# Layer 1 of two attention layers: where the maxima are turned, and how the last two chunks are summed

## The chip, the cores and the metric

One core of one Trainium2 chip runs the whole kernel. The metric is the device time of one execution in microseconds; the figure to compare is the median of several executions. In every profile PE is the matrix engine (PEld its weight loads), DVE the vector engine, ACT the scalar engine, POOL the GpSimd engine, and SP the engine that issues most DMAs. L905 means line 905 of the kernel before.

## What is computed

The input is x of shape (2, 256, 64, 64), in float32. Two attention layers follow each other. Layer 0 normalises, attends with 4 heads of 16, scales and passes through a sigmoid; the change does not touch it. Layer 1 is:

```python
def _L1_conv_ref(x, w_qkv, b_qkv, w_out, b_out):
    b, c, h, w = x.shape
    head_dim = c // HEADS                     # 4 heads of 64
    qkv = jnp.einsum('oc,bchw->bohw', w_qkv, x) + b_qkv[None, :, None, None]
    qkv = qkv.reshape(b, HEADS, 3 * head_dim, h * w)
    q, k, v = jnp.split(qkv, 3, axis=2)
    attn = jax.nn.softmax(jnp.einsum('bhdn,bhdm->bhnm', q, k) * scale, axis=-1)
    out = jnp.einsum('bhnm,bhdm->bhnd', attn, v).reshape(b, c, h, w)
    return jnp.einsum('oc,bchw->bohw', w_out, out) + b_out[None, :, None, None] + x
```

There are 4096 positions for each of 2 images, so each head has a score matrix of 4096 by 4096.

## The kernel before

**Units, steps, chunks.** Layer 1 is cut into 32 units. A unit is one image, one pair of heads and one block of 512 queries. It goes over all 4096 keys in 32 chunks of 128 keys, two chunks a step, so a unit has 16 steps, numbered 0 to 15 here, and layer 1 has 512 steps. One tile of a chunk is 128 keys by 1024: 512 queries for each of the two heads.

**The life of a chunk.** `score` multiplies keys by queries into a pair of PSUM banks (L888; two such pairs). `keep` takes the running maximum over chunks on DVE (`rmax`, L905) and copies the scores to an SBUF tile `raw` on ACT (L906). The tiles `raw` are a ring of 26 buffers. Eleven steps later (`LAG`) `shift` subtracts the queries' maxima on DVE (L977), `weigh` takes the exponential on ACT (L989) and adds the weights into a running total on POOL (L1001; L999 for the first two chunks of a half). A step after that `gather` multiplies the weights by the values on PE (L1030). A buffer of the ring is free for chunk t+26 once POOL's addition and PE's weighing of chunk t are over.

**Halves and maxima.** The 32 chunks are two halves of 16, and each half has a maximum of its own. When a half is complete (step 8 for the first, step 0 of the next unit for the second) `turn_max` transposes `rmax` on PE, one head at a time, into the single spare bank `misc` (L918), and `fold` reduces it on DVE (L935), sends it to DRAM and reads it back, spread over all partitions, as a row. `place_shift` copies the row into PSUM on ACT (L959) two steps later. One chunk of each half is shifted by POOL instead of DVE (L966).

**Sums.** POOL adds 30 of the 32 chunks of a unit. The last two are summed by PE: `gather` of the last chunk multiplies both by ones (L1043), in step 11 of the next unit, into two column groups of the spare bank. `total` in step 12 adds POOL's two totals to the same bank (L1060): the first half into column groups at 0 and 32, the second half onto the last chunks at 64 and 96. `keep_total` copies the bank out in step 13 (L1068) and sends it through DRAM with five DMAs, so that it comes back with queries on partitions. `add_sums` on POOL multiplies the first half by the ratio of the two maxima's exponentials (L1151) and adds the second (L1152). `factors` and `rows` turn the sums into factors and apply them in steps 0 and 1 of the unit after.

**Projections beside it.** The first 24 units also project keys and values that a later pair of heads needs, a quarter at a time: keys in steps 2 to 5, values in steps 6, 7, 9 and 10 (`next_values`, L835), kept by `store_values` on ACT (L844) in steps 8 and 11. The last eight units do the output projection in the same places (`project_out`, `output`, L812, L1200), with two additions on POOL (L1206). Queries of the next unit are projected in steps 13 and 14. All of these, the turned maxima and the sums share the one spare bank.

**What sets the order.** The order is written by hand. A table maps a step and a place to calls (`at`, run by `hung`), and the main loop runs the places of a step in this order: scores of both chunks, exponential left from the step before, `start`, `early`, keep of the first chunk, shift and exponential of an older chunk, `early end`, keep of the second chunk, weighing of two chunks, `late`, `late end`, shift of the second older chunk, `end`. Every engine works through its own instructions in that order. The main loop before:

```python
            scores = [score(c) for c in pair] if inside else []
            if 0 <= t - LAG - 1 < END:
                weigh(pair[1] - 2 * LAG - 2)
            hung(t, "start")
            hung(t, "early")
            if inside:
                keep(pair[0], scores[0])
```

Of the kernel before, what the change touches and what calls it, by code (L numbers as in the profile page):

```python
# [8 lines left out]
F32 = mybir.dt.float32  # L9
AF = mybir.ActivationFunctionType  # L10
ALU = mybir.AluOpType
# [3 lines left out]
P = 128  # L15
# [11 lines left out]
def conv_attention_kernel(  # L27
# [205 lines left out]
    with own0:  # L233
# [417 lines left out]
        def misc(name):  # L651
            return small_bank[0](name)
# [118 lines left out]
    with (  # L771
# [26 lines left out]
        sum1 = {  # L798
            u: dram.tile([NG * 2, NB], F32, tag="sum_{}_{}_{}".format(*u), name=f"sum_{u}")
            for u in units  # L800
        }
        first, begun, late = {}, set(), {}


# [217 lines left out]
        def gather(t):  # L1022
            u = b, g, j = units[t // NM]
            m = t % NM
            n = m // GS
            if m % GS == 0:
                avs1[u, n] = psv.tile([P, NB], F32, tag="av", name=f"av1_{b}_{g}_{j}_{n}")
            v = vs[b, g, m // PB]
            for k in range(2):
                seq(nc.tensor.matmul(  # L1030
                    avs1[u, n][k * D1 : (k + 1) * D1, :], v[:, m % PB, k, :], raws[t][:, k, :],
                    start=(m % GS == 0), stop=(m % GS == GS - 1),
                ))
            if on_tensor(t) and t % 2 == 1 and t != 2 * END - 1:
                late_sums((t - 1, t) if on_tensor(t - 1) else (None, t))
            elif t == 2 * END - 2:
                late_sums((t, t + 1))
            if m == NM - 1 and u != units[-1]:
                srows[u] = misc(f"sum1_{b}_{g}_{j}")
                for i in (t - 1, t):  # L1040
                    for k in range(2):
                        r = D1 * (NG - 1) + 32 * k
                        seq(nc.tensor.matmul(  # L1043
                            srows[u][r : r + 32, :], ones[:, :32], raws[i][:, k, :],
                            start=(i < t), stop=False, skip_group_check=True,
                        ))
            raws.pop(t - 2, None)
            if m % GS == GS - 1:
                a = l1.tile([P, NB], F32, tag="avs", name=f"avs1_{b}_{g}_{j}_{n}")
                seq(nc.scalar.copy(a, avs1.pop((u, n))))  # L1050
                avs1[u, n] = a

        def total(u):


            b, g, j = u
            for n in range(NG):
                for k in range(2):
                    r = D1 * n + 32 * k
                    seq(nc.tensor.matmul(  # L1060
                        srows[u][r : r + 32, :], ones[:, :32], accs[u, n][:, k, :],
                        start=(n < NG - 1), stop=True, skip_group_check=True,
                    ))

        def keep_total(u):
            b, g, j = u
            row = l1.tile([P, NB], F32, tag="kv", name=f"srow_{b}_{g}_{j}")
            seq(nc.scalar.copy(  # L1068
                row.rearrange("p (a m i) -> p a i m", m=P, i=2),
                srows[u].rearrange("p (a i m) -> p a i m", m=P, i=2),  # L1070
            ))
            for m in range(2 * NG):
                nc.sync.dma_start(out=sum1[u][m : m + 1, :], in_=row[32 * m : 32 * m + 1, :])
            s = small.tile([P, NG, 2, PB], F32, tag="sums1", name=f"sums1_{b}_{g}_{j}")
            nc.sync.dma_start(
                out=s.rearrange("p n k (a i) -> p (n k a) i", i=2),
                in_=sum1[u].rearrange("m (a p i) -> p (m a) i", p=P, i=2),
            )
            srows[u] = s
# [141 lines left out]

        for n, u in enumerate(units):
            b, g, j = u
            t0 = n * US
# [6 lines left out]
            if n < len(units) - NJ:  # L1233
                to = (*units[n + NJ][:2], j)
                at(max(t0 - 1, 0), "start", lambda to=to: fetch(("kv", *to), x1[to[0]][to[2]]))
                for q in range(4):
                    at(t0 + 2 + q, "late", lambda to=to, q=q: next_keys(*to, q))
                    at(t0 + (6, 7, 9, 10)[q], "late", lambda to=to, q=q: next_values(*to, q))
                at(t0 + 6, "start", lambda to=to: store_keys(*to))
                for i, step in enumerate((t0 + 8, t0 + 11)):  # L1240
                    at(step, "start", lambda to=to, i=i: store_values(*to, i))

                t1 = (n // NJ * NJ + NJ - 1) * US
                at(t1 + 2 * j + 2, "start", lambda to=to: load_keys(*to))
                at(t1 + 2 * j + 3 + LAG, "start", lambda to=to: load_values(*to))
            for k in range(NG):
                t1 = t0 + (k + 1) * GS // 2
                places = ("early", "early" if (u, k) == (units[-1], NG - 1) else "late")
                for i, place in enumerate(places):
                    at(t1, place, lambda u=u, k=k, i=i: turn_max(u, k, i))  # L1250
                    at(t1, f"{place} end", lambda u=u, k=k, i=i: fold(u, k, i))
                at(t1 + 2, "end", lambda u=u, k=k: place_shift(u, k))
            t1 = t0 + US + GS // 2
            if u != units[-1]:
                at(t1 + 4, "late", lambda u=u: total(u))
                at(t1 + 5, "start", lambda u=u: keep_total(u))
                at(t1 + 1, "late", lambda u=u: lose(u))
                at(t1 + 7, "late end", lambda u=u: add_sums(u))
                at(t1 + 8, "end", lambda u=u: factors(u))
                for place, k in (("early", 1), ("late", 0)):  # L1260
                    at(t1 + 9, place, lambda u=u, k=k: turn_sums(u, k))
                    at(t1 + 9, f"{place} end", lambda u=u, k=k: rows(u, k))
            else:
                at(END + 1, "late", lambda u=u: last_lost(u))
                at(END + 4, "early", lambda u=u: late_sums((None, None)))
                at(END + 4, "early end", lambda u=u: keep_late(0))
                at(END + 5, "early", lambda u=u: turn_late(0))
                at(END + 5, "early end", lambda u=u: add_late(u, 0))
                at(END + 6, "early", lambda u=u: turn_sums(u, 0))
                at(END + 6, "early end", lambda u=u: first_rows(u))  # L1270
                at(END + LAG, "late", lambda u=u: turn_late(1))
                at(END + LAG, "late", lambda u=u: add_late(u, 1))
                at(END + LAG, "late", lambda u=u: turn_sums(u, 1))
                at(END + LAG, "late", lambda u=u: last_rows(u))
            if n >= len(units) - NJ:
                b0 = B - 2
                at(t0 - 1, "start", lambda b0=b0, j=j: fetch_output(b0, j))
                for o in range(CC):
                    for q in range(4):
                        step = t0 + ((2, 3, 4, 5), (6, 7, 9, 10))[o][q]  # L1280
                        at(step, "late", lambda b0=b0, j=j, o=o, q=q: project_out(b0, j, o, q))
                at(t0 + 6, "start", lambda b0=b0, j=j: output(b0, j, 0, 2))
                for part, step in enumerate((t0 + 8, t0 + 11)):
                    at(step, "start", lambda b0=b0, j=j, part=part: output(b0, j, 1, part))


# [77 lines left out]
        for t in range(max(t for t, _ in extras) + 1):  # L1364
            inside, behind = 0 <= t < END, 0 <= t - LAG < END
            pair = (2 * t, 2 * t + 1)
            scores = [score(c) for c in pair] if inside else []
            if 0 <= t - LAG - 1 < END:
                weigh(pair[1] - 2 * LAG - 2)
            hung(t, "start")  # L1370
            hung(t, "early")
            if inside:
                keep(pair[0], scores[0])
            if behind:
                shift(pair[0] - 2 * LAG)
                weigh(pair[0] - 2 * LAG)
# [80 lines left out]
```

## Time and profile before

| | |
|---|---|
| median of 3 executions | 4640.9 us (4640.56 to 4641.03) |
| the profiled execution, its own time | 4640.95 us |
| span in its profile, first to last instruction | 4639.2 us |
| first scores of layer 1 | 2057.8 us from the start of the span |
| a unit of layer 1 | 78.9 us (78.88 to 79.01 for units 2 to 30) |
| granted clock of PE | 0.996 |

A line of the groups reads: line, engine, operation, output<-inputs, shape, count, then busy time in us and mean ns of one, then the engine's idle time just before and what ended it. A line of the timeline reads: start, duration, engine, line, operation, output<-inputs, count, and in brackets the idle time before and what ended it. A line of the waits reads: who waited, for whom, us in total, how often, the longest. Times of one unit are given from that unit's first score.

### The profile page before, as it was taken

The numbers are of one execution on the slowest core, as the hardware profiler recorded it, in microseconds if no ns is written. First come the engines' busy times: TensorE is split into PE (matmuls) and PEld (weight loads), VectorE is DVE, ScalarE is ACT, GpSimd is POOL, SyncE is SP. The second block draws the span as 40 slices with busy tenths as digits, with TensorE's granted clock in tenths as the row PEclk, the third lists the DMA queues.
The fourth block names the chain that finished last, engine by engine and source line by source line (L and its number), as shares of the span: only waits on it lengthen the run. The fifth ranks groups of instructions, "written<-read, shape, count | busy, mean of one in ns | idle before, by whom it ended". The sixth has DMA issues, their size and how long they took to land. (4 is left out here: it accounts for less than half of the span.)

```text
span 4639.2 us, 73122 instructions
## 1 busy us (share of the span) xinstructions
PE 4499.0 (97%) x28490; PEld 1511.6 (33%) x28490; DVE 3833.4 (83%) x4443; ACT 3439.9 (74%) x4588; POOL 2514.8 (54%) x1307
## 2 busy tenths in 40 slices
PE   8999999999999999999999999999999999999998
PEld 3433333333333333333333333333333333323332
DVE  6777777777777777529999999999999999999997
ACT  3266666666666666668888888888888888888885
POOL 5300000000000000008999999999999999999995
PEclk9999999999999999999999999999999999999999
DMA  3100000000000000121111221111211112111213
GB/s 101 39 4 20 20 20 15 15 15 15 15 15 15 15 13 13 33 75 40 35 42 35 55 56 39 37 40 42 71 42 36 39 33 62 51 53 37 53 40 112
DMA packets 190475, 174.84 MB, mean 38 GB/s; under 512 B 120232, under 2 KB 121064, under 8 KB 190128
## 3 DMA queue, kind: packets, MB, share of 16 engines
q1 hardware_dynamic: 188272, 169.58, 13.2%
q8 instruction: 223, 3.65, 0.3%
q14 instruction: 124, 1.02, 0.1%
q10 hardware_dynamic: 1856, 0.59, 0.1%
HBM read 127.65 MB, written 42.48 MB: 37 GB/s over the span
## 5 line engine op out<-in xcount | busy, mean ns | idle before, releaser
L1001 POOL TENSOR_TENSOR acc<-acc,raw 128x1024 f32<-128x1024 f32 x821 | 1950.4, 2376 | 80.1 <-ACT raw L989 30.7
L402 DVE TENSOR_REDUCE mx<-a 128x1 f32<-128x512 f32 x2048 | 1315.5, 686 | 449.9 <-PE a L398 448.8
L439 ACT ACTIVATE p<-s 128x512 f32<-128x512 f32 x2048 | 1108.3, 595 | 702.5 <-PE a L398 367.6
L905 DVE TENSOR_TENSOR rmax<-s,rmax 128x1024 f32<-128x1024 f32 x960 | 1171.6, 1220 | 99.7 <-PE s L888 89.6
L436 PE MATMUL s<-q,kT 32*128 32x512 f32 x4096 | 1218.8, 640 | 0.0
L888 PE MATMUL s<-q,k 64*128 64x512 f32 x4096 | 1120.3, 637 | 98.1 <-ACT raw L906 93.2
L906 ACT COPY raw<-s 128x1024 f32<-128x1024 f32 x1024 | 1035.6, 1011 | 240.8 <-DVE rmax L905 163.5
L977 DVE TENSOR_TENSOR raw<-raw,shift 128x1024 f32<-128x1024 f32 x961 | 1160.7, 1212 | 3.3 <-ACT shift L959 1.8
L989 ACT ACTIVATE raw<-raw 128x1024 f32<-128x1024 f32 x1024 | 1084.9, 1060 | 62.8 <-DVE raw L977 27.7
L398 PE MATMUL a<-kT,q 32*128 32x512 f32 x4096 | 1129.8, 643 | 1.4 <-DVE mx L402 1.3
L1030 PE MATMUL av<-raw,v 128*64 128x512 f32 x4096 | 1007.4, 607 | 4.2 <-ACT raw L989 2.5
L451 PE MATMUL av<-p,v 128*32 128x256 f32 (+1 forms) x7904 | 650.1, 399 | 0.6 <-ACT avs L465 0.6
L501 POOL TENSOR_TENSOR f<-f,dyn 128x16 f32<-128x16 f32 x15 | 3.3, 221 | 1028.2 <-DVE f L500 1028.2
L888 PEld LDWEIGHTS s<-q,k 64*128 64x128 f32 x4096 | 316.8, 185 | 678.7 <-ACT raw L906 487.0
L436 PEld LDWEIGHTS s<-q,kT 32*128 32x128 f32 x4096 | 397.7, 183 | 426.3 <-issue 392.1
L1030 PEld LDWEIGHTS av<-raw,v 128*64 128x64 f32 x4096 | 242.4, 136 | 650.8 <-issue 476.4
L451 PEld LDWEIGHTS av<-p,v 128*32 128x32 f32 x7904 | 157.7, 108 | 751.5 <-issue 737.3
L552 POOL TENSOR_SCALAR res<-res 128x1024 f32<-128x1024 f32 x16 | 16.7, 1044 | 660.3 <-ACT res L551 660.3
L398 PEld LDWEIGHTS a<-kT,q 32*128 32x128 f32 x4096 | 305.2, 184 | 31.4 <-DVE mx L402 18.2
L999 POOL TENSOR_TENSOR acc<-raw,raw 128x1024 f32<-128x1024 f32 x64 | 152.1, 2376 | 60.9 <-ACT raw L989 60.3
L966 POOL TENSOR_TENSOR raw<-raw,row 128x1024 f32<-128x1024 f32 x63 | 151.7, 2407 | 37.9 <-DMA row<-neg 37.9
L935 DVE TENSOR_REDUCE negs<-rt 128x4 f32<-128x512 f32 x126 | 87.0, 690 | 58.8 <-PE rt L918 58.8
(338 smaller groups left out, 1913.5 us busy)
## 6 DMA issues: line engine op xcount, KB each, us to landing
row<-neg SPq DMA_DIRECT2D x64, 512.0 KB
x<-in_x_dram SPq DMA_DIRECT2D x16, 512.0 KB
res<-in_x_dram SPq DMA_DIRECT2D x16, 512.0 KB
x<-res SPq DMA_DIRECT2D x16, 512.0 KB
att<-rows SPq DMA_DIRECT2D x62, 128.0 KB
kd<-k1s SPq DMA_DIRECT2D x24, 256.0 KB
vd<-v1s SPq DMA_DIRECT2D x24, 256.0 KB
k<-kd SPq DMA_DIRECT2D x24, 256.0 KB
```

The source lines that it names most:

```text
L398: seq(nc.tensor.matmul(ps, qs0[u][r, bass.ts(i, P)], kTs[b][r, bass.ts(m, NB)], start=True, stop=True,))
L402: seq(nc.vector.tensor_reduce(mxs[u][:, i * H + h, m : m + 1], ps, AX.X, ALU.max))
L436: seq(nc.tensor.matmul(ps, kTs[b][r, bass.ts(m, P)], qs0[u][r, :], start=True, stop=True))
L439: seq(nc.scalar.activation(pt[:, k, :], ps, AF.Exp, scale=D0**-0.5))
L451: seq(nc.tensor.matmul(avs[u][32 * h : 32 * h + 32, cols], vs0[b][:, m, 32 * h : 32 * h + 32], pts[t, h // 2][:, h % 2, cols], start=(m == ...
L888: seq(nc.tensor.matmul(ps[:, k, :], ks[b, g, m // PB][r, bass.ts(m % PB, P)], qs1[u][r, :], start=True, stop=True,))
L905: seq(nc.vector.tensor_tensor(rmax[u, n], ps, before, ALU.max))
L906: seq(nc.scalar.copy(raw, ps))
L977: seq(nc.vector.tensor_tensor(raws[t], raws[t], shifts[u, t % NM // GS], ALU.add))
L989: seq(nc.scalar.activation(p, p, AF.Exp, scale=D1**-0.5))
L1001: seq(nc.gpsimd.tensor_tensor(accs[u, n], accs[u, n], p, ALU.add))
L1030: seq(nc.tensor.matmul(avs1[u, n][k * D1 : (k + 1) * D1, :], v[:, m % PB, k, :], raws[t][:, k, :], start=(m % GS == 0), stop=(m % GS == GS ...
```

## The change

It has three parts, all in layer 1, and all units but the last take part.

1. *Maxima.* The first head's maxima are turned in a new place, `between`, between the two scores of the step, and folded in a new place, `kept`, ahead of the shift of the older chunk. The second head's are turned in `early end`, ahead of the second keep and of the weighing, where they stood behind the weighing; their fold stays in `late end`. The second half of the last unit keeps its places.
2. *Values.* The second quarter of the values (in the last eight units, of the output) moves from step 7 to step 6, and its keeping from step 8 to step 7.
3. *Sums.* The last two chunks are summed into four column groups of a bank of their own turn (`csums`), and not into two. An added `keep_chunks` in step 12 copies that bank out and sends it through DRAM with five DMAs. `total` in step 12 then has four column groups without anything to add onto. `add_sums` has two more additions on POOL.

The diff, cut to its core:

```diff
@@ gather
             if m == NM - 1 and u != units[-1]:
-                srows[u] = misc(f"sum1_{b}_{g}_{j}")
-                for i in (t - 1, t):
+                csums[u] = misc(f"csum1_{b}_{g}_{j}")
+                for i in range(2):
                     for k in range(2):
-                        r = D1 * (NG - 1) + 32 * k
+                        r = D1 * i + 32 * k
                         seq(nc.tensor.matmul(
-                            srows[u][r : r + 32, :], ones[:, :32], raws[i][:, k, :],
-                            start=(i < t), stop=False, skip_group_check=True,
+                            csums[u][r : r + 32, :], ones[:, :32], raws[t - 1 + i][:, k, :],
+                            start=True, stop=True,
                         ))
@@ total
+            srows[u] = misc(f"sum1_{b}_{g}_{j}")
...
-                        start=(n < NG - 1), stop=True, skip_group_check=True,
+                        start=True, stop=True,
@@ keep_rows takes the place of keep_total's body and is called twice
-        def keep_total(u):
+        def keep_rows(ps, to, tag, name):
+            row = l1.tile([P, NB], F32, tag="kv", name=f"srow_{name}")
             seq(nc.scalar.copy(
                 row.rearrange("p (a m i) -> p a i m", m=P, i=2),
-                srows[u].rearrange("p (a i m) -> p a i m", m=P, i=2),
+                ps.rearrange("p (a i m) -> p a i m", m=P, i=2),
             ))
...
+        def keep_chunks(u):
+            csums[u] = keep_rows(csums[u], csum1[u], "csums", "c_{}_{}_{}".format(*u))
+
+        def keep_total(u):
+            srows[u] = keep_rows(srows[u], sum1[u], "sums1", "{}_{}_{}".format(*u))
@@ add_sums
             seq(nc.gpsimd.tensor_tensor(s[:, 0], s[:, 0], lost, ALU.mult))
+            c = csums.pop(u)
+            seq(nc.gpsimd.tensor_tensor(s[:, 0], s[:, 0], c[:, 0], ALU.add))
+            seq(nc.gpsimd.tensor_tensor(s[:, 1], s[:, 1], c[:, 1], ALU.add))
             seq(nc.gpsimd.tensor_tensor(s[:, 1], s[:, 1], s[:, 0], ALU.add))
@@ the table
-                    at(t0 + (6, 7, 9, 10)[q], "late", lambda to=to, q=q: next_values(*to, q))
+                    at(t0 + (6, 6, 9, 10)[q], "late", lambda to=to, q=q: next_values(*to, q))
-                for i, step in enumerate((t0 + 8, t0 + 11)):
+                for i, step in enumerate((t0 + 7, t0 + 11)):
                     at(step, "start", lambda to=to, i=i: store_values(*to, i))
...
-                places = ("early", "early" if (u, k) == (units[-1], NG - 1) else "late")
-                for i, place in enumerate(places):
-                    at(t1, place, lambda u=u, k=k, i=i: turn_max(u, k, i))
-                    at(t1, f"{place} end", lambda u=u, k=k, i=i: fold(u, k, i))
+                if (u, k) == (units[-1], NG - 1):
+                    places = ("early", "early end", "early", "early end")
+                else:
+                    places = ("between", "kept", "early end", "late end")
+                for i in range(2):
+                    at(t1, places[2 * i], lambda u=u, k=k, i=i: turn_max(u, k, i))
+                    at(t1, places[2 * i + 1], lambda u=u, k=k, i=i: fold(u, k, i))
...
+                at(t1 + 4, "start", lambda u=u: keep_chunks(u))
                 at(t1 + 4, "late", lambda u=u: total(u))
                 at(t1 + 5, "start", lambda u=u: keep_total(u))
...
-                        step = t0 + ((2, 3, 4, 5), (6, 7, 9, 10))[o][q]
+                        step = t0 + ((2, 3, 4, 5), (6, 6, 9, 10))[o][q]
@@ the main loop
-            scores = [score(c) for c in pair] if inside else []
+            scores = [score(pair[0])] if inside else []
             if 0 <= t - LAG - 1 < END:
                 weigh(pair[1] - 2 * LAG - 2)
             hung(t, "start")
+            hung(t, "between")
+            if inside:
+                scores.append(score(pair[1]))
             hung(t, "early")
             if inside:
                 keep(pair[0], scores[0])
+            hung(t, "kept")
```

More of the change, by code (lines that the diff above doesn't have):

```diff
@@ L797, in conv_attention_kernel @@
         }
[L798 to L801, printed above, removed]
+        sum1, csum1 = (
+            {
+                u: dram.tile([4, NB], F32, tag="{}_{}_{}_{}".format(s, *u), name=f"{s}_{u}")
+                for u in units
+            }
+            for s in ("sum", "csum")
+        )
+        csums = {}
         first, begun, late = {}, set(), {}
@@ L1061, in total @@
                         srows[u][r : r + 32, :], ones[:, :32], accs[u, n][:, k, :],
-                        start=(n < NG - 1), stop=True, skip_group_check=True,
+                        start=True, stop=True,
                     ))
-        def keep_total(u):
-            b, g, j = u
-            row = l1.tile([P, NB], F32, tag="kv", name=f"srow_{b}_{g}_{j}")
+        def keep_rows(ps, to, tag, name):
+            row = l1.tile([P, NB], F32, tag="kv", name=f"srow_{name}")
             seq(nc.scalar.copy(
                 row.rearrange("p (a m i) -> p a i m", m=P, i=2),
-                srows[u].rearrange("p (a i m) -> p a i m", m=P, i=2),
+                ps.rearrange("p (a i m) -> p a i m", m=P, i=2),
             ))
-            for m in range(2 * NG):
-                nc.sync.dma_start(out=sum1[u][m : m + 1, :], in_=row[32 * m : 32 * m + 1, :])
-            s = small.tile([P, NG, 2, PB], F32, tag="sums1", name=f"sums1_{b}_{g}_{j}")
+            for m in range(4):
+                nc.sync.dma_start(out=to[m : m + 1, :], in_=row[32 * m : 32 * m + 1, :])
+            s = small.tile([P, 2, 2, PB], F32, tag=tag, name=f"sums1_{name}")
             nc.sync.dma_start(
                 out=s.rearrange("p n k (a i) -> p (n k a) i", i=2),
-                in_=sum1[u].rearrange("m (a p i) -> p (m a) i", p=P, i=2),
+                in_=to.rearrange("m (a p i) -> p (m a) i", p=P, i=2),
             )
-            srows[u] = s
+            return s
+        def keep_chunks(u):
+            csums[u] = keep_rows(csums[u], csum1[u], "csums", "c_{}_{}_{}".format(*u))
+        def keep_total(u):
+            srows[u] = keep_rows(srows[u], sum1[u], "sums1", "{}_{}_{}".format(*u))
             seq(nc.scalar.activation(losts[u], losts[u], AF.Exp, scale=D1**-0.5))
@@ L1279, in conv_attention_kernel @@
                     for q in range(4):
-                        step = t0 + ((2, 3, 4, 5), (6, 7, 9, 10))[o][q]
+                        step = t0 + ((2, 3, 4, 5), (6, 6, 9, 10))[o][q]
                         at(step, "late", lambda b0=b0, j=j, o=o, q=q: project_out(b0, j, o, q))
                 at(t0 + 6, "start", lambda b0=b0, j=j: output(b0, j, 0, 2))
-                for part, step in enumerate((t0 + 8, t0 + 11)):
+                for part, step in enumerate((t0 + 7, t0 + 11)):
                     at(step, "start", lambda b0=b0, j=j, part=part: output(b0, j, 1, part))
```

## The prediction

> **What bounds the kernel now.** I read the page, then one repeating piece of layer 1 at a time. Layer 1 starts its first scores at 2057.8 us, and 30 of its 32 units repeat every 78.9 to 79.0 us. So the question is what sets 78.9. The page and two such units (the second is one of the last eight, which also project the output):
>
> ```profile
> span 4639.2 us, 73122 instructions
> PE 4499.0 (97%) x28490; PEld 1511.6 (33%) x28490; DVE 3833.4 (83%) x4443; ACT 3439.9 (74%) x4588; POOL 2514.8 (54%) x1307
> ...
> 3143.78:3222.67 78.89, 75.82 (x362) 24.82 (x360) 73.97 (x69) 69.73 (x76) 74.16 (x37) 1.00 0.13 37
> 4090.80:4169.77 78.97, 75.80 (x346) 23.95 (x344) 74.00 (x69) 69.94 (x76) 76.55 (x39) 1.00 0.17 44
> ```
>
> Columns of the last two: length, then busy us of PE, PEld, DVE, ACT, POOL. In layer 1 four engines are each busy 70 to 77 of 79 us; POOL's 54% on the page is an average over a layer 0 that hardly uses it. The waits between 2500 and 4500 us (some 25 units) and the groups say who holds whom:
>
> ```profile
> ACT raw L906 <- DVE rmax L905: 122.5, 176, 0.9
> DVE rmax L905 <- PE s L888: 69.4, 154, 1.6
> DVE negs L935 <- PE rt L918: 47.5, 77, 0.7
> POOL acc L999 <- ACT raw L989: 40.3, 20, 2.3
> POOL acc L1001 <- ACT raw L989: 19.0, 26, 1.0
> ...
> L1001 POOL TENSOR_TENSOR acc<-acc,raw 128x1024 f32<-128x1024 f32 x661 | 1570.4, 2376 | 58.6 <-ACT raw L989 19.0 <-POOL acc L1001 0.6
> L1043 PE MATMUL sum<-raw,ones 128*32 128x512 f32 x200 | 47.8, 598 | 0.0
> L1060 PE MATMUL sum<-acc,ones 128*32 128x512 f32 x200 | 26.6, 605 | 0.0
> ```
>
> DVE loses 47.5/25.4 = 1.9 us a unit to the transposes of the maxima and 2.7 to late scores. POOL waits for exponentials in one place only. The timeline of the unit that starts at 3143.78 shows where (step 4, the folds in step 8, POOL in step 12):
>
> ```profile
> 3167.13 2.39 POOL L1001 TENSOR_TENSOR acc<-acc,raw 128x1024 f32<-128x1024 f32 x1
> 3168.32 1.22 DVE L905 TENSOR_TENSOR rmax<-s,rmax 128x1024 f32<-128x1024 f32 x1
> 3169.63 1.02 ACT L906 COPY raw<-s 128x1024 f32<-128x1024 f32 x1
> ...
> 3185.93 0.65 PE L918 MATMUL rt<-ident,rmax 128*128 128x128 f32 x4 [0.25 <-ACT v1s L844]
> 3186.70 0.69 DVE L935 TENSOR_REDUCE negs<-rt 128x4 f32<-128x512 f32 x1
> 3188.38 0.66 PE L918 MATMUL rt<-ident,rmax 128*128 128x128 f32 x4
> 3189.07 0.69 DVE L935 TENSOR_REDUCE negs<-rt 128x4 f32<-128x512 f32 x1 [0.55 <-PE rt L918]
> ...
> 3205.97 2.37 POOL L999 TENSOR_TENSOR acc<-raw,raw 128x1024 f32<-128x1024 f32 x1 [2.26 <-ACT raw L989]
> 3209.09 2.37 POOL L1001 TENSOR_TENSOR acc<-acc,raw 128x1024 f32<-128x1024 f32 x1 [0.75 <-ACT raw L989]
> ```
>
> Times below are from the unit's start. POOL restarts at 65.31 (3209.09) on the exponential of chunk 2 and then never rests until step 12 of the next unit. The ring `raw` has 26 buffers, so the second copy of step 4 (chunk 9) takes the buffer of the previous unit's chunk 15, whose addition ends at 25.74 (3169.52). The copy starts at 25.85. The maximum that it also waits for ends at 25.76: both arrive together. POOL has **0.1 us of slack** there. The unit that starts at 2985.88 proves the tie: its addition ends at 26.06, its copy starts at 26.10, and that unit takes 79.00.
>
> **What the Trainium skill says.** "PSUM — Partial Sum Buffer", PSUM bank collisions: two engines may not be on one bank and quadrant at once, reads included; so the copy L906 starts after the maximum L905 ends (here about 0.1 us after), and score, maximum, copy form a chain per pair of banks. "TensorEngine Tiling (Array Packing)", Tiling Modes: at 128x32 there are four independent column tiles. The trace agrees: the sums of L1060 use four, those of L1043 two, and eight records begin within 0.99 against 1.84 us. "Trainium Kernel Development and Optimization", Performance Expectations, calls matmul busy time a bad metric, because matmuls are pipelined. Agreed: a score that does not wait has a pitch of 0.96 us though its records span 1.13; I use pitches.
>
> **The change, part by part.** Pitches from this trace: score 0.96 (1.06 after a wait), weighing of two chunks 1.77 to 1.87, turn 0.59, quarter of values 0.44 to 0.54, DVE maximum or shift 1.14, fold 0.60 (0.69 to its end), copy 1.01, exponential 1.06. A maximum starts 1.18 after its score, a copy 1.32 after its maximum, the next score of the bank 0.05 after the copy.
>
> Step 0 (maxima of the second half). Before: second score 1.85, turn, weighing, turn, next score at 5.95. After: the first turn runs at 0.96 to 1.55 while PE waits for the banks until 1.85 anyway; fold at 1.8, its shift behind it; second turn at 2.9, weighing to 5.25, next score about 5.27. **Gain 0.68**.
>
> Step 6. The second quarter of values adds 0.44 to PE, so step 7's score would be 0.44 late; the keeping of the half (0.35 on ACT) moves to step 7 and fits (the same holds for the output's projection in the last eight units, 0.46). If the last copy of step 5 starts 0.27 earlier, as it does when ACT was held by POOL and not by DVE (copy 28.18, exponential 29.2, copy 30.26 instead of 30.53), 0.17 remains: maxima of step 7 at 36.31 instead of 36.13, of step 8 at 40.85 instead of 40.66.
>
> Step 8 (first half's maxima). First turn free as in step 0. The second turn needs the one spare bank, so it waits for the first fold's end: 40.85+1.14+0.69 = 42.68, while PE has been free since 42.0. Turn to 43.3, weighing, next score at 45.17 (before 45.19): **gain 0**. The 0.25 wait of the turn for the keeping of values goes, and is replaced by this one. Until step 11 nothing moves.
>
> Step 11. Eight records of sums shrink by 1.84-0.99 = 0.85: scores of step 12 at 59.70 instead of 60.54. But ACT is busy without a gap to 62.09 (shift, exponentials, copies, `avs`), and the added row copy (0.63, as L1068) stands in front of step 12's first copy: 62.72 instead of 63.03; exponential of chunk 2 at 63.73 instead of 64.11. POOL restarts at 64.94: **gain 0.37**. The second row copy in step 13 follows with 0.85 of ACT work; chunk 4's exponential then comes 0.08 too late for POOL. On DVE and PE 0.30 of the 0.85 arrives at the next unit.
>
> Added sums: two POOL additions, 128x8, 0.20 each; by the pitches of L1151 and L1152 (0.28 when the second needs the first, else 0.16) **+0.44**, bounds 0.32 and 0.56. They stand between POOL's restart and chunk 15. In step 12 the sums of the running totals need the spare bank that this copy empties: it ends at 62.7, PE comes at 63.5. The copy's own buffer, of tag `kv`, and the next one's were last read by stores issued in steps 6 and 11; the later has 9 us to land. The five extra DMAs of the rows go through SP in step 12, ahead of step 13's five; nobody waits for them before POOL's sums at 3.5 of the next unit, so nothing; a late landing would stop POOL's whole queue.
>
> Sum. PE and DVE alone would come to step 4 earlier by 0.68+0.30 = 0.98. They then wait in the ring, because POOL comes at: restart −0.37, +0.08, additions +0.44, slack −0.1, that is +0.05 to +0.07. The rest of the loop is unchanged. So a unit takes 78.97 instead of 78.90: 22 units × 0.07 = 1.5. In the last eight POOL also adds the output (76.55 busy, 0.05 of idle before L999), and its restart gains 0.2 and not 0.37: 8 × 0.2 = 1.6. Together +3.1. The profiled execution took 4640.95, 1.75 around its span; the median is 4640.9. Forecast **4644**.
>
> **Rivals.** *Slower, 4653.* The second turn's wait for the fold is paid. Its place is steps 6 to 8: if step 5's last copy does not start 0.27 earlier, all 0.44 of the extra quarter reaches the first fold, and the weighing behind the second turn ends 0.28 later. Then (0.07+0.28)×22+(0.2+0.28)×8 = 11.5, so about 4653. For it: PE then idles 0.7 to 1 us before the turn. Against: ACT in step 5 starts from the ring and not from DVE. It decides from 0.15 of extra delay.
>
> *Faster, 4611 to 4631, middle 4621.* POOL does not hold the loop: its additions cost nothing there, or the restart comes earlier than I find (the addition of chunks 0 and 1 allows 64.6, that is 0.67). Then up to 0.98 a unit is kept: 30 × 0.98 = 29. POOL's work would allow that: it idles 3.0 us a unit. Against it: the two waits that meet at 25.8.
>
> *The change does not do what it says*, four column groups run no faster: excluded by L1060.
>
> **Numbers.** POOL's loop as computed, 4644 (own range 4635 to 4650): 0.47. Slower rival, 4650 to 4665: 0.33. Faster rival: 0.20. The 8-in-10 range leaves out the lower half of the faster case and the top of the slower: 4622 to 4660. A measurement of this kernel tells 0.2% (9.3 us) from no change: faster below 4631.6, 0.20; slower above 4650.2, 0.33; within 0.47.
>
> **What would show it.** Right: copies waiting for POOL additions in step 4 (now (19.0+1.2)/25.4 = 0.8 a unit, L999 counted) rise to about 1.5; the wait of folds for turns goes from 1.9 to under 0.5 while maxima wait more for scores; PE waits before the second turn for the fold; four-group sums at 0.133 us a record; step 0 about 0.7 shorter, step 11 about 0.8, steps 2 to 4 longer. Wrong: units below 78.6 with no copy waiting for POOL, or the weighing of step 8 pushed past 45.5.

## The result

The changed kernel takes **4625.99 us** (median of 8 executions, 4625.53 to 4628.36) against 4640.66 for the kernel before in the same measurement (4639.59 to 4641.64): a ratio of 0.997, with a 95% interval of 0.996 to 0.9979. That is 14.7 us less. The forecast was 4644, 3 us more. So the time lies inside the range, but on the side that had a chance of 0.20.

From here on line numbers are those of the changed kernel: maximum L909, copy of the scores L910, exponential L993, first addition L1003, further additions L1005, turn L922, fold L939, sums of the last chunks L1048, of the totals L1066, copy of the rows L1074. In the section on the experiments they are those of the kernel in question.

The same first lines of the page:

```profile
span 4624.1 us, 73518 instructions
PE 4464.2 (97%) x28490; PEld 1497.1 (32%) x28490; DVE 3830.0 (83%) x4443; ACT 3448.6 (75%) x4619; POOL 2527.6 (55%) x1369
```

And the two units that answer to those of before, one in the middle of layer 1 and one of the last eight (length, then busy us of PE, PEld, DVE, ACT, POOL):

```profile
3136.26:3214.69 78.43, 74.74 (x364) 24.34 (x362) 73.88 (x69) 70.09 (x77) 74.61 (x39) 1.00 0.15 38
4077.80:4156.60 78.80, 74.79 (x346) 23.59 (x344) 74.00 (x69) 70.20 (x77) 77.00 (x41) 1.00 0.18 44
```

A unit takes 78.43 where it took 78.89, though ACT and POOL are busier in it (70.09 and 74.61 against 69.73 and 74.16). From the first score of layer 1 to the first score of its last unit the changed kernel is 14.9 us shorter: 10.5 of it in 22 units of 0.48 each, 2.2 in the first two, 2.2 in the seven behind. The stretches ahead of layer 1 and from the last unit on differ by 0.5 (longer) and 0.7 us (shorter).

The waits between 2500 and 4500 us show which wait went and which came:

```profile
DVE rmax L909 <- PE s L892: 99.4, 155, 1.0
ACT raw L910 <- DVE rmax L909: 76.4, 157, 0.8
POOL acc L1003 <- ACT raw L993: 35.1, 18, 2.0
ACT raw L910 <- POOL acc L1005: 26.1, 22, 1.4
PE rt L922 <- DVE negs L939: 15.2, 25, 0.6
ACT raw L910 <- POOL acc L1003: 8.4, 24, 0.4
```

The wait of the folds for the turns (47.5 us before) is gone. POOL's further additions no longer wait for an exponential (19.0 before). Copies of the scores now wait 34.5 us for POOL, 1.35 a unit. So the forecast's first sign of being wrong came only by half: the units are below 78.6, but copies do wait for POOL. A few lines of the first of these units' timeline, in step 4, in step 8 and in step 12:

```profile
3160.29 2.38 POOL L1005 TENSOR_TENSOR acc<-acc,raw 128x1024 f32<-128x1024 f32 x1
3160.37 1.22 DVE L909 TENSOR_TENSOR rmax<-s,rmax 128x1024 f32<-128x1024 f32 x1
3162.71 1.01 ACT L910 COPY raw<-s 128x1024 f32<-128x1024 f32 x1 [1.16 <-POOL acc L1005]
...
3178.63 0.68 DVE L939 TENSOR_REDUCE negs<-rt 128x4 f32<-128x512 f32 x1
3179.37 0.65 PE L922 MATMUL rt<-ident,rmax 128*128 128x128 f32 x4 [0.63 <-DVE negs L939]
...
3198.82 2.39 POOL L1003 TENSOR_TENSOR acc<-raw,raw 128x1024 f32<-128x1024 f32 x1 [1.95 <-ACT raw L993]
3200.02 1.13 ACT L993 ACTIVATE raw<-raw 128x1024 f32<-128x1024 f32 x1
3201.29 4.86 POOL L1005 TENSOR_TENSOR acc<-acc,raw 128x1024 f32<-128x1024 f32 x2
```

The copy of chunk 9 has its maximum at 3161.59 and starts only at 3162.71, 0.04 after POOL's addition of chunk 15 (3162.67): the ring holds it, now by itself. And in step 12 POOL's second addition follows the first without a gap; before, it waited 0.75 for the exponential of chunk 2.

### The profile page after: what moved, and what is told of

The parts are those of the page before. It is cut to its first block, busy times and chain, and to the rows that moved or that the text cites. A ratio compares the mean times of both kernels' runs of the same rounds, so it can differ in the third digit from the quotient of the medians.

```text
span 4624.1 us, 73518 instructions
## 1 busy us (share of the span) xinstructions
PE 4464.2 (97%) x28490; PEld 1497.1 (32%) x28490; DVE 3830.0 (83%) x4443; ACT 3448.6 (75%) x4619; POOL 2527.6 (55%) x1369
## 5 line engine op out<-in xcount | busy, mean ns | idle before, releaser
L1005 POOL TENSOR_TENSOR acc<-acc,raw 128x1024 f32<-128x1024 f32 x821 | 1951.1, 2376 | 58.9 <-ACT raw L993 7.4
L909 DVE TENSOR_TENSOR rmax<-s,rmax 128x1024 f32<-128x1024 f32 x960 | 1172.3, 1221 | 138.1 <-PE s L892 126.7
L910 ACT COPY raw<-s 128x1024 f32<-128x1024 f32 x1024 | 1038.0, 1014 | 203.6 <-DVE rmax L909 106.1
L993 ACT ACTIVATE raw<-raw 128x1024 f32<-128x1024 f32 x1024 | 1088.7, 1064 | 77.5 <-DVE raw L981 47.9
L1003 POOL TENSOR_TENSOR acc<-raw,raw 128x1024 f32<-128x1024 f32 x64 | 152.5, 2384 | 52.7 <-ACT raw L993 52.7
L922 PE MATMUL rt<-ident,rmax 128*128 128x128 f32 x504 | 82.6, 286 | 20.1 <-DVE negs L939 19.0
```

The source lines that it names most:

```text
L909: seq(nc.vector.tensor_tensor(rmax[u, n], ps, before, ALU.max))
L910: seq(nc.scalar.copy(raw, ps))
L993: seq(nc.scalar.activation(p, p, AF.Exp, scale=D1**-0.5))
L1005: seq(nc.gpsimd.tensor_tensor(accs[u, n], accs[u, n], p, ALU.add))
```

## Where the time came from

Two events cut the unit in two, so that each half can be compared: the copy of chunk 9, which the ring releases, and POOL's restart, the addition of chunk 2 in step 12. In us (medians of units 2 to 22):

| | copy of chunk 9 to restart | restart to next copy of chunk 9 | unit |
|---|---|---|---|
| before | 39.46 | 39.44 | 78.90 |
| the forecast's working | 39.09 | 39.86 | 78.95 |
| after | 38.59 | 39.84 | 78.43 |

The second half is POOL alone, and the forecast has it to 0.02. The first half runs over ACT, and there 0.50 a unit is missing from the forecast; 0.50 times 30 units is 15 of the 18 us by which it was off. ACT's queue from the exponential of chunk 1 to that of chunk 2, first before and then after:

```profile
3204.80 1.08 ACT L989 ACTIVATE raw<-raw 128x1024 f32<-128x1024 f32 x1
3206.81 1.01 ACT L906 COPY raw<-s 128x1024 f32<-128x1024 f32 x1 [0.92 <-DVE rmax L905]
3207.88 1.06 ACT L989 ACTIVATE raw<-raw 128x1024 f32<-128x1024 f32 x1
```

```profile
3197.65 1.10 ACT L993 ACTIVATE raw<-raw 128x1024 f32<-128x1024 f32 x1
3198.61 0.68 ACT L1074 COPY srow_c<-csum 128x512 f32<-128x512 f32 x1
3199.12 1.07 ACT L910 COPY raw<-s 128x1024 f32<-128x1024 f32 x1
3200.02 1.13 ACT L993 ACTIVATE raw<-raw 128x1024 f32<-128x1024 f32 x1
```

The three starts lie 0.96, 0.51 and 0.90 apart, 2.37 in all, where the durations read 1.10, 0.68 and 1.07. The forecast took the exponential's duration, 0.63 and 1.01, together 2.70. These records of ACT overlap where the next instruction is ready, and the forecast added durations. The kernel before shows it as well: in its step 11 a copy starts at 3203.44 and lasts 1.01, and the next record starts at 3204.33, after 0.89.

## The experiments

Every kernel is compared with the kernel before in the same measurement, on the same chip. "Unit" is the median of units 2 to 23.

| kernel | median us | before us | ratio (95%) | unit |
|---|---|---|---|---|
| changed | 4625.99 | 4640.66 | 0.9970 (0.9960 to 0.9979) | 78.43 |
| ring27_after | 4613.39 | 4640.16 | 0.9944 (0.9929 to 0.9959) | 77.85 |
| ring27_before | 4644.37 | 4640.16 | 1.0009 (1.0000 to 1.0018) | 78.90 |
| max_values | 4630.10 | 4640.16 | 0.9979 (0.9972 to 0.9986) | 78.63 |
| sums_only | 4628.95 | 4640.16 | 0.9976 (0.9967 to 0.9986) | 78.47 |
| pool_adds_doubled | 4635.22 | 4639.32 | 0.9990 (0.9981 to 0.9999) | 78.72 |
| values_back | 4659.43 | 4639.32 | 1.0044 (1.0029 to 1.0059) | 79.55 |
| sums_on_dve | 4737.69 | 4639.32 | 1.0212 (1.0197 to 1.0228) | 81.97 |
| ring27_sums_on_dve | 4735.57 | 4639.32 | 1.0210 (1.0195 to 1.0225) | 81.97 |
| adds_left_out | 4611.42 | 4638.98 | 0.9941 (0.9925 to 0.9958) | 77.95 |
| row_copy_doubled | 4642.37 | 4638.98 | 1.0008 (0.9999 to 1.0016) | 79.03 |
| ring27_adds_joined | 4611.77 | 4638.98 | 0.9943 (0.9928 to 0.9958) | 77.84 |
| one_operand_in_psum | 4622.56 | 4639.73 | 0.9962 (0.9948 to 0.9976) | 78.36 |

The theory after the result: POOL's loop through the ring of 26 buffers sets the unit, as forecast, and the restart came 0.5 earlier than forecast. The rival, the first branch of the forecast's own faster case: the ring and POOL do not hold the unit, and the gain is what PE and DVE save.

**One more buffer in the ring, in both kernels.** The space comes from another tile's tag.

```diff
-bufs=2 * LAG + 4
+bufs=2 * LAG + 5
-fetch(("ao", b, j), att[b][:, bass.ts(j, NB)], "ao", 1, l1)
+fetch(("ao", b, j), att[b][:, bass.ts(j, NB)])
-fetch_last(4, l1, "ao")
+fetch_last(4, l1, "rmax", 2)
```

> The changed kernel with 27 buffers in the ring and not 26 (the projection's input shares a tag to make room). Theory, POOL's loop sets the unit through the ring: with one buffer more, the copy of chunk 9 waits for the addition of chunk 14, which ends 2.4 us earlier, so the 1.0 us that PE and DVE are early by is kept: a unit of 77.5 to 77.9 us and not 78.43, some 4600 to 4612 us, and hardly a copy that waits for POOL in step 4. Rival, PE and DVE set the unit: no change, 4624 to 4628.

> The kernel before with 27 buffers in the ring. Theory: before the change the ring and DVE arrive together within 0.1 us, so a looser ring gives at most 0.1 us a unit: 4637 to 4641 us. Rival, the ring has nothing to do with it: 4640.7. Were the ring the only bound before too, 4620 or less.

The changed kernel goes down by another 12 us: its unit is as expected (77.85), its time lies 1.4 above the expected range. The kernel before does not go down. Its unit stays at 78.90, but its time lies 3.4 above the expected range: in the profiled execution 4.0 of the 4.2 us more lie behind the first score of the last unit (157.08 in place of 153.10). The same edit gives fetches of the last units other tiles; why that stretch is longer was not tested, and the units ahead of it are not touched.

The copy of chunk 9 with 27 buffers starts as soon as its maximum is there, and does not wait for POOL's addition of chunk 15, which begins at 3154.41 and ends at 3156.78; between 2500 and 4500 us copies wait 0.4 us for POOL in place of 34.5:

```profile
3154.54 1.22 DVE L909 TENSOR_TENSOR rmax<-s,rmax 128x1024 f32<-128x1024 f32 x1
3155.85 1.01 ACT L910 COPY raw<-s 128x1024 f32<-128x1024 f32 x1
```

So the ring held the changed kernel's unit, by 0.58 (78.43 less 77.85), and the kernel before was held within 0.1 by both, as the forecast had read. This rules the rival out. In units 26 to 30 POOL's own work takes over (78.5 to 78.8): in units 26 to 29 no gap of POOL is longer than 0.12 us.

**The parts alone.** max_values has parts 1 and 2, sums_only has part 3.

```diff
 max_values: turns and folds in "between", "kept", "early end", "late end"; values (6, 6, 9, 10), kept in t0 + 7; sums as before
 sums_only: csums, keep_chunks, four column groups, two more additions; turns, folds and values as before
```

> Parts 1 and 2 alone on the kernel before (maxima between and behind the scores, half the values in step 6), sums as before. Theory: POOL's loop from its restart in step 12 to chunk 15 is as before, so the 0.7 us of step 0 ends in the ring, and what is left is the slack of 0.1 and 0.2 from steps 5 to 9: a unit of 78.6 to 78.8, 4632 to 4638 us. Rival, PE and DVE set the unit: 0.7 a unit is kept, 4618 to 4622.

> Part 3 alone on the kernel before (last chunks on four column groups, a copy and two POOL additions more). Theory: POOL restarts about 0.65 us earlier in step 12 and pays 0.47 us for its additions, so 0.2 to 0.3 us a unit is kept: 4631 to 4637 us. Rival, PE and DVE set the unit: the 0.85 us of PE in step 11 less the added copy, 0.3 to 0.8 a unit, 4617 to 4632.

The halves of the unit tell what each brings:

| | copy of chunk 9 to restart | restart to next copy of chunk 9 | unit |
|---|---|---|---|
| before | 39.46 | 39.44 | 78.90 |
| max_values | 39.24 | 39.39 | 78.63 |
| sums_only | 38.66 | 39.81 | 78.48 |
| both (changed) | 38.59 | 39.84 | 78.43 |

Each takes about 2 us less than its range allowed. The time of sums_only even lies in the range of its rival (4617 to 4632); what speaks against that rival is not this time but the run with 27 buffers, and that here too the copy of chunk 9 starts 0.03 after POOL's addition and some 0.5 after its maximum. Together the parts bring 14.7 us, less than 10.1 and 11.2. The first half shrinks by 0.22 and 0.80 alone and by 0.87 together, so 0.15 is the same gain twice. As soon as POOL holds the copy of chunk 9, by either part, ACT works off a queue behind it: from this copy to the second copy of step 9 it took 24.09 before, 23.87 with max_values, 23.94 with sums_only, 23.87 with both. In the second half the slack before POOL's addition, too, can be used only once: 0.05 less and 0.37 more alone, 0.40 more together.

**POOL's additions, twice and not at all.**

```diff
 pool_adds_doubled
             seq(nc.gpsimd.tensor_tensor(s[:, 1], s[:, 1], c[:, 1], ALU.add))
+            seq(nc.gpsimd.tensor_tensor(spare, s[:, 0], c[:, 0], ALU.add))
+            seq(nc.gpsimd.tensor_tensor(spare, spare, c[:, 1], ALU.add))
 adds_left_out
-            seq(nc.gpsimd.tensor_tensor(s[:, 0], s[:, 0], c[:, 0], ALU.add))
-            seq(nc.gpsimd.tensor_tensor(s[:, 1], s[:, 1], c[:, 1], ALU.add))
```

> The changed kernel with two more additions of 128x8 on POOL beside the two that the change added (into a tile that nothing reads). Theory, POOL's stretch from its restart in step 12 to chunk 15 sets the unit: 0.44 to 0.5 us a unit more, 78.9 us and 4637 to 4642 us, though POOL idles 2 us a unit. Rival, POOL has room and PE and DVE set the unit: no change, 4626.

> The changed kernel without the two added POOL additions (the last two chunks' sums are fetched and never added: they are left out of the result). Theory (POOL's loop through the ring sets 78.43): the two additions take 0.30 to 0.47 a unit on POOL between its restart and chunk 15, and the way over PE and ACT would allow 77.85, so all of it comes back: 4611 to 4618. Rival (the additions lie in POOL's idle time, as in the faster rival of the forecast): 4624 to 4629.

Without the additions the second half of the unit is 39.37 and not 39.84, and the first half stays 38.58: **0.48 a unit** for two additions of 128x8, all of it on the path, as the forecast's 0.44 said. Two further ones cost 0.30 (40.14), less than expected, and the time lies 1.8 below its range. The starts of POOL's small operations with the two further ones say why:

```profile
3142.40 0.20 POOL L1163 TENSOR_TENSOR sums<-sums,lost 128x8 f32<-128x8 f32 x1
3142.68 0.20 POOL L1165 TENSOR_TENSOR sums<-sums,sums_c 128x8 f32<-128x8 f32 x1
3142.84 0.20 POOL L1166 TENSOR_TENSOR sums<-sums,sums_c 128x8 f32<-128x8 f32 x1
3143.00 0.20 POOL L1168 TENSOR_TENSOR spare<-sums,sums_c 128x8 f32<-128x8 f32 x1
3143.28 0.20 POOL L1169 TENSOR_TENSOR spare<-spare,sums_c 128x8 f32<-128x8 f32 x1
3143.44 0.20 POOL L1170 TENSOR_TENSOR sums<-sums 128x8 f32<-128x8 f32 x1
```

An operation that needs the result just ahead of it starts 0.28 later, any other 0.16. The further two put 0.16 and 0.28 in, and L1170, which needs the result just ahead in the changed kernel, no longer does: 0.32 more in all. The small operations of POOL are paid in full because POOL has no wait between its restart and chunk 15 that could hide them: in unit 10 its only gap above 0.12 us is the 1.96 ahead of L1003.

**The row copy in step 12, twice.** It undoes the earlier exponential.

```diff
+            if tag == "csums":
+                seq(nc.scalar.copy(
+                    row.rearrange("p (a m i) -> p a i m", m=P, i=2),
+                    ps.rearrange("p (a i m) -> p a i m", m=P, i=2),
+                ))
```

> The changed kernel with the added copy of the sums' rows on ACT in step 12 made twice; its pitch on ACT is 0.51 us. Theory: the exponential of chunk 2 ends 0.04 us before POOL is free for it, so the restart comes 0.45 later, and the unit grows by as much: 4636 to 4641. Rival (the restart is POOL's own, and ACT's queue in step 12 has room, as the forecast had it when it let the restart follow the exponential by 0.2): under 0.15 a unit, 4624 to 4631.

```profile
3206.41 0.66 ACT L1074 COPY srow_c<-csum 128x512 f32<-128x512 f32 x1
3207.10 0.65 ACT L1079 COPY srow_c<-csum 128x512 f32<-128x512 f32 x1
3207.63 1.02 ACT L910 COPY raw<-s 128x1024 f32<-128x1024 f32 x1
3208.53 1.07 ACT L993 ACTIVATE raw<-raw 128x1024 f32<-128x1024 f32 x1
3209.74 2.37 POOL L1005 TENSOR_TENSOR acc<-acc,raw 128x1024 f32<-128x1024 f32 x1 [0.73 <-ACT raw L993]
```

POOL waits 0.73 again, the first half is 39.24 (0.65 more), the second nearly unchanged (39.80), and the whole gain is gone: 4642.37, slightly more than expected. The two copies take 0.69 and 0.53, and not 0.51 each. They write the same tile, which may be why the first pair does not overlap; that was not tested. It shows how thin the forecast was cut: 0.7 us in ACT's queue at this place is the difference between faster and no change.

**The second quarter of the values back in step 7**, kept in step 8, everything else changed.

```diff
-at(t0 + (6, 6, 9, 10)[q], "late", ...
+at(t0 + (6, 7, 9, 10)[q], "late", ...
-for i, step in enumerate((t0 + 7, t0 + 11)):
+for i, step in enumerate((t0 + 8, t0 + 11)):
```

> The changed kernel with the second quarter of the values back in step 7 and its keeping in step 8. By the prediction's step 6 this saves up to 0.17 us a unit: 4621 to 4626 us. By the theory now, the quarter in step 6 costs nothing, and in step 8 the first turn, now between the scores, must wait for the spare bank until the values are kept, with the second score behind it: 0.5 to 1.5 us a unit more, 4640 to 4670 us.

```profile
3190.64 1.13 PE L892 MATMUL s<-q,k 64*128 64x512 f32 x4
3192.77 0.35 ACT L848 COPY v1s<-v1p 128x256 f32<-128x256 f32 x1
3193.18 0.65 PE L922 MATMUL rt<-ident,rmax 128*128 128x128 f32 x4 [1.41 <-ACT v1s L848]
3193.76 1.13 PE L892 MATMUL s<-q,k 64*128 64x512 f32 x4
```

The turn stands between the two scores, finds the spare bank full of values until 3193.1, and the second score waits behind it: 3.12 after the first and not 1.74. A unit is 1.1 us longer, as the theory had it; the saving that the forecast's step 6 would give did not come. So part 2 is what makes the place `between` free, and in the changed kernel its cost is hidden: the second copy of step 9 stands 23.87 after the copy of chunk 9, before 24.09. With 27 buffers, where the ring does not hold that copy, it stands 24.32 after it, so there the cost shows.

**The sums' four operations on DVE**, with 26 and with 27 buffers, to take them out of POOL's loop.

```diff
-            seq(nc.gpsimd.tensor_tensor(s[:, 0], s[:, 0], lost, ALU.mult))
+            seq(nc.vector.tensor_tensor(s[:, 0], s[:, 0], lost, ALU.mult))
 (the three additions likewise)
```

> The changed kernel with the four small operations of the sums on DVE and not on POOL. Theory: POOL reaches chunk 15 0.9 us earlier, the ring lets go, and the unit falls to what PE, DVE and ACT allow, 77.8 to 78.0 us as with 27 buffers; the last eight units, which POOL's work bounds, gain too: 4604 to 4613 us. Rival, POOL not the bound and DVE nearly so: DVE takes 0.7 us a unit more, 4626 to 4645.

> The changed kernel with both: 27 buffers and the sums' small operations on DVE. Theory: in the first 24 units POOL no longer binds, so about the 77.85 us of 27 buffers alone; in the last eight POOL's own work binds at 78.7 us with 27 buffers alone and falls by up to 0.9: 4603 to 4611 us. Rival, DVE pays for its operations: 4613 to 4630.

Both expectations failed by more than 120 us, their rivals by more than 90, and a unit takes 3.5 more. The timeline of DVE, and POOL's over the same time:

```profile
3343.60 0.52 DVE L1163 TENSOR_TENSOR sums<-sums,lost 128x8 f32<-128x8 f32 x1
3344.16 0.17 DVE L1165 TENSOR_TENSOR sums<-sums,sums_c 128x8 f32<-128x8 f32 x1
3344.24 2.31 DVE L1166 TENSOR_TENSOR sums<-sums,sums_c 128x8 f32<-128x8 f32 x1
3346.59 0.17 DVE L1167 TENSOR_TENSOR sums<-sums 128x8 f32<-128x8 f32 x1
```

```profile
3339.27 7.26 POOL L1005 TENSOR_TENSOR acc<-acc,raw 128x1024 f32<-128x1024 f32 x3
```

POOL's three additions, which this line merges, end at 3341.64, 3344.10 and 3346.53. The two long operations of DVE end at 3344.12 and 3346.55: each ends with an addition of POOL, and so it is in all 31 units that have them, to 0.03. The arrival of the sums is not the reason: L1165 has read both fetched tiles in 0.17 when L1166 starts. The Trainium skill has a reason on "SBUF — State Buffer", Who interferes with whom: a DVE instruction with two inputs in SBUF contends with a GpSimd instruction that reads SBUF, because the second input comes through the read interface that the two share; the page calls the lock on the shared ports exclusive and says that the order of issue decides who blocks. Here the two long operations began during an addition of POOL (these start at 3341.72 and 3344.18), the two short ones did not. To test it, one operand was taken from PSUM:

```diff
-            seq(nc.vector.tensor_tensor(s[:, 0], s[:, 0], lost, ALU.mult))
+            bank = shifts[units[units.index(u) + 1], 0][:, :, :PB]
+            seq(nc.vector.tensor_tensor(s[:, 0], s[:, 0], bank, ALU.mult))
 (the three additions likewise)
```

> The four operations of the sums on DVE as in the kernel with the sums on DVE, but each takes its second operand from the bank of the shifts in PSUM in place of the fetched sums: the ratio, the second totals and the last chunks are left out of the result. Theory (an operation of DVE with both operands in SBUF waits until the addition that POOL has begun is over): the four take 0.17 each or a little more for PSUM, the 2.3 and 0.5 us are gone, POOL's loop is shorter by all four of its small operations, and the time falls to 4606 to 4616. Rival (DVE waits for something else at that place, the sums' arrival or its own queue): about 4737 as before.

```profile
L1166 DVE TENSOR_TENSOR sums<-sums,shift 128x8 f32<-128x8 f32 x26 | 4.2, 163 | 0.9
L1168 DVE TENSOR_TENSOR sums<-sums,shift 128x8 f32<-128x8 f32 x26 | 4.2, 163 | 0.9
L1167 DVE TENSOR_TENSOR sums<-sums,shift 128x8 f32<-128x8 f32 x26 | 4.1, 156 | 0.0
L1165 DVE TENSOR_TENSOR sums<-sums,shift 128x8 f32<-128x8 f32 x26 | 4.0, 153 | 0.0
```

These are groups between 2500 and 4500 us; the last number ahead of the second bar is the mean in ns. All four take 153 to 163 ns, and 115 us of the time are gone. So it is the two operands in SBUF that make them long. The size was missed by 7 us: 4622.56 against 4606 to 4616. The copy of chunk 9 now starts 0.3 after POOL's addition and 0.09 after its maximum, so the way over DVE holds the unit (78.36). DVE carries the four operations in the first 1.4 us of the next unit, and there the copy of chunk 9 stands at 25.93, with 27 buffers at 25.42. With both operands in SBUF the sums are far cheaper on POOL, even inside the loop that sets the time; with one in PSUM the place makes little difference (78.36 against 78.43).

**27 buffers and the additions joined to one.**

```diff
-            seq(nc.gpsimd.tensor_tensor(s[:, 0], s[:, 0], c[:, 0], ALU.add))
-            seq(nc.gpsimd.tensor_tensor(s[:, 1], s[:, 1], c[:, 1], ALU.add))
+            seq(nc.gpsimd.tensor_tensor(s, s, c, ALU.add))
```

> 27 buffers in the ring, and the two added additions of 128x8 joined to one of 128x16. Theory: with 27 buffers POOL's loop does not hold the first units (77.85), only the last five, where POOL's own work is the bound; one addition fewer gives these 0.15 to 0.2 each and nothing elsewhere: 4611 to 4614, against 4613.4 with 27 buffers alone. Rival (POOL's loop still holds all units with 27 buffers): 0.15 to 0.2 in 30 units, 4607 to 4609.

It takes 27.2 us off the kernel before; with 27 buffers alone it was 26.8, and the intervals overlap. The units agree with the theory: 77.84 as before the joining, and about 78.6 in place of 78.75 at the end. Of the versions that leave nothing out, those with 27 buffers and the sums on POOL are the fastest.

## Why the forecast was wrong, step by step

**Right: what sets the unit.** POOL's loop through the ring, with both waits meeting at 25.8 in the kernel before. The 27 buffers show it for the changed kernel, and show the small slack before.

**Right: POOL's side.** Restart to the copy of chunk 9 was worked out as 39.86 and is 39.84: the additions at 0.44 (0.48), the slack of 0.1 used up. Only the 0.08 for chunk 4's exponential did not come, since that one now has time.

**Right: PE's operations.** Four column groups take 26.6 us for 200 records, 0.133 each, and step 11 fell from 6.18 to 5.32. In step 8 the second turn waits for the first fold with PE idle (0.63), as worked out. Steps 0 and 15 together are 0.58 shorter, for 0.68. The held copy shows in step 5 (5.53, before 4.51) and not, as forecast, in steps 2 to 4: it is the second copy of step 4, and only the score of the step after needs its bank.

**Wrong: the size of the restart's gain in step 11** ("gain 0.37"). It is 0.87, made of two terms of ACT's queue, both sized by durations. The forecast lists 1.01 for a copy and 1.06 for an exponential among its pitches, but these are durations.

- From the exponential of chunk 1 to that of chunk 2 the forecast has 2.70 after the change; it is 2.37. The kernel before has 3.08 (1.06 to 1.08 for each record and 0.92 of waiting). So 0.71 is gained here, for 0.38.
- Up to the exponential of chunk 1 the forecast has no gain: in step 6 "0.17 remains", and step 8 has "gain 0". The trace has 34.94 from the copy of chunk 9 to that exponential (3162.71 to 3197.65), before 35.17 (3169.63 to 3204.80). The step behind it is the last copy of step 5, expected 0.27 earlier: it is 0.5 earlier (4.18 after the copy of chunk 9, before 4.68), because copy and exponential off a queue start 0.91 and 0.96 apart and were counted at 1.02 and 1.06. That pays for the whole quarter of 0.44.

ACT behind the copy of chunk 9 (3162.71) in the changed kernel, up to the last copy of step 5:

```profile
3163.61 1.06 ACT L993 ACTIVATE raw<-raw 128x1024 f32<-128x1024 f32 x1
3165.02 1.02 ACT L910 COPY raw<-s 128x1024 f32<-128x1024 f32 x1 [0.34 <-POOL acc L1003]
3165.93 1.06 ACT L993 ACTIVATE raw<-raw 128x1024 f32<-128x1024 f32 x1
3166.89 1.00 ACT L910 COPY raw<-s 128x1024 f32<-128x1024 f32 x1
```

The other kernels separate the two terms (medians of units 2 to 22, from one start to the next):

| | copy of chunk 9 to exponential of chunk 1 | on to exponential of chunk 2 | on to restart |
|---|---|---|---|
| before | 35.19 | 3.07 | 1.20 |
| max_values | 34.96 | 3.08 | 1.20 |
| sums_only | 35.03 | 2.37 | 1.27 |
| both (changed) | 34.95 | 2.37 | 1.27 |
| row_copy_doubled | 34.95 | 3.08 | 1.20 |
| ring27_after | 35.40 | 2.36 | 1.27 |

The second column falls with part 3 alone, and the row copy made twice gives it back whole. The first falls wherever the ring holds the copy of chunk 9, by either part, and is longer than before where 27 buffers let go of it.

Together the two terms are 0.71 + 0.23 = 0.94. POOL takes 0.88 of it in this unit, because it is then busy with chunks 0 and 1 until 3201.21. This is the bound of 0.67 that the forecast named in its faster rival ("the restart comes earlier than I find"), moved by the 0.23: the case was seen and given 0.20, together with one that was false.

**The slower rival** did not come, since its condition (step 5's last copy not 0.27 earlier) was missed on the other side.

**The last eight units** were to lose 0.2 each, with 0.2 gained at the restart; units 25 to 29 gain 0.2 to 0.3. Before, POOL waited 0.65 there for the exponential of chunk 2, and this wait went whole. In units 26 to 29 POOL now has no gap above 0.12 us: its own work sets them.

The Trainium skill would have warned of the failed step: "ScalarE: Activation LUTs", What ACT_TABLE_LOAD costs, gives an overlap of about 93 ns for one ACTIVATE right behind another. The traces agree: in the kernel before, an exponential of 1.06 that has an ACTIVATE of the queries' projection behind it sees that one start 0.96 after its own start, in all 52 cases between 2500 and 4500 us. Here a copy behind an exponential does the same. The forecast took pitches for PE and durations for ACT.

## What to carry to other kernels

Where a loop over several engines sets the time, cut it at two events that every version has and compare the halves: one table then tells which engine's side was mis-sized, when the total tells nothing. Build every queue from the start-to-start spacing of records that did not wait, for each engine and not only for PE: 0.1 us a record, some five records long, was here the difference between no change and 15 us. And when a trace shows two waits that end together, expect a change on one side to bring what the other allows, and look for the resource that joins them: one more buffer was worth 12 us after this change and brought nothing before it.

## What the hardware showed that was not expected

- Four operations of 128x8 on DVE cost 3.5 us a unit when both operands were in SBUF and POOL was adding: single ones lasted 0.52 and 2.31 us, each to the end of POOL's addition, where 0.17 is the length alone. With one operand in PSUM all took 0.15 to 0.17.
- Two copies on ACT that write the same tile start 0.69 apart (0.66 long), the next copy, to another tile, 0.53 later. A record of ACT that is ready starts about 0.1 before the end of an exponential or a copy of 128x1024 ahead of it (0.96 after one of 1.06, 0.89 to 0.91 after one of 1.01).
- The price of a small operation on POOL depends on what stands ahead of it: 0.28 to the next start if that one needs its result, 0.16 if not, while every record reads 0.20.
